# A two-layer graph attention network on one core: the order of loads at the start and ahead of layer 2's attention vectors

## The chip, the cores and the metric

The kernel runs on one core of one Trainium2 chip. The metric is the device time of one execution in microseconds. A core has a matrix engine (TensorE, PE in the profile, with its weight loads as PEld), a vector engine (VectorE, DVE), a scalar engine (ScalarE, ACT), a general one (GpSimd, POOL) and a synchronising one (SyncE, SP). Each runs its own instructions in program order, and they wait for each other by semaphores. Here SP's queue issues the plain loads and stores and the transposes by DMA, and POOL's queue the DMAs that add what they load to what stands in the destination (accumulating DMAs).

## The reference

512 nodes with 768 features, 16,896 edges (8,192 pairs in both directions and 512 loops), sorted by destination. Two graph attention layers, then a residual and a layer norm, all in float32:

```
def gat_layer(x, W, a_s, a_d, b, edge_index, concat):
    h = (x @ W).reshape(n, H, C)
    alpha_s = einsum('nhc,hc->nh', h, a_s);  alpha_d = einsum('nhc,hc->nh', h, a_d)
    e = leaky_relu(alpha_s[src] + alpha_d[dst], 0.2)
    e = exp(e - segment_max(e, dst)[dst])
    alpha = e / (segment_sum(e, dst)[dst] + 1e-16)
    return segment_sum(h[src] * alpha[:, :, None], dst).reshape(n, H * C) + b
h = elu(gat_layer(x, W1, a_src1, a_dst1, b1))      # 8 heads of 768
y = gat_layer(h, W2, a_src2, a_dst2, b2)           # 6144 to 768, one head
out = layernorm(x + y)
```

## The kernel before, in words

**The whole.** The edges are turned into a dense 512 x 512 matrix of counts (`cnt`), so that the attention of a head is a dense softmax with counts as weights and its message sum a dense product. Layer 1 is worked head by head: the projection x W1[h], the logits, the softmax, the attention's product, ELU, and the head's share of layer 2's projection, which is added into `h2`. All big products are done in float32 by schemes that trade multiplications for additions: 7 products of halves in place of 8 (`by_halves`, P1 to P7), or 15 of thirds. The sums of weights that these need are made on DVE, or by accumulating DMAs on POOL, the sums of activations on DVE. The order of all instructions on all engines is written out by hand (`manual_schedule`); no scheduler moves them.

**The projection of head 0 and its loads (lines 232 to 266).** The tiles `w1r` hold W1[0] as a lower and an upper half of rows (lo, hi), each with a left and a right half of columns (L, R). The loop at L251 and L252 issues the right halves: first block and rest of lo R, then hi R (576 KB). `sums_by_dma` (L254 to L264) then loads, on SP, the bases of the sums t2 (w1t2, from hi R) and t4 (w1t4, from hi L), 576 KB each (L259), and gives back two additions for POOL: t2 += t1 (L261) and t4 += t2 (L262). The attention rows a_s, a_d of head 0 follow (`load_a`, L224). `weight_sums` (L557), called in the second batch below, makes t1 = lo L + lo R on DVE (L559), then issues the first addition, a third accumulating load that makes lo R + hi R in place (L561), and the second addition. In the program's order the products (`multiply`, L426) of head 0 are P1, P2, P6, P7, P4, P5, P3 in pairs of halves of rows (i = 0, 1), six matmuls of the profile each; head 0 itself is worked in an order of its own, by a list of items. The same helper is called again for the last block of W2 with the same tiles (slot "w1").

**The front end (L273 to L384).** `keep_warm` issues matmuls on zeros so that TensorE is not idle while the first loads come. `nodes` is an iota; `offsets` (L366) a table of small numbers copied from it by DVE. The edge indices arrive as int32 (`idx_i`), are cast to float on DVE (`idx_f`, L367) and transposed on PE (L373), after six transposes of x (`turn_x`, L311), whose results ACT copies into `xT` (L312). From the transposed indices DVE and POOL make the parts of the one-hots (`fold`, `low`, `rel`, `two`, `weight`, L377 to L384).

**The counting (L732 to L888).** The count matrix is a sum of products of one-hots: 32 destinations by 256 sources for each chunk of 128 edges (`count`, L782). Source one-hots are made on DVE by comparison (L756, "ours") or on ACT by a sign (L754, "theirs"); destination one-hots on DVE for a quarter of the chunks at a time (`destinations`, L734 and L735). The loop over nine batches (L814 to L888) runs these beside the products of head 0: in each, first the quarter's destinations, then the source one-hots for the next batch, the list `extra` of sums and logits, some products with their emptying from PSUM, and at the end the counting matmuls of this batch. The list at L814 gives how many one-hots of each kind a batch takes. `inside` (L738) sums up how many edges lie in the block that their chunk is taken to cover; the sum decides whether a general pass is run afterwards.

**The step from head 0 to head 2's projection (h = 0 of the loop at L1229 on).** During the attention product of head 0 and layer 2's product, SP's queue holds, in this order: `load_w1(2)`, `load_a(2)` (a_s and a_d of head 2, each a row spread over 128 partitions, 384 KB, L224), the four loads of `attended(0)` (L1211 to L1214: 128 rows of W2's last block, a_src2 and a_dst2), then the transposes by DMA of the normalised weights (`turn_out`, L969), and then the three parts of `load_second(1)` (L153, L147, L161). Tiles with one buffer are reused, so that a load of a_d waits until DVE has done its last logit with the old a_d (L435). `turn_out` scales a tile on ACT, splits its 16-bit halves on ACT (L967) and issues the transpose on SP; `turn_in` joins the halves on ACT (L972). Then follows the projection of head 2 (L426, in `by_halves`): its P1 is emptied from PSUM by ACT (L465), its P2 by ACT too (L466), the others by DVE (L467 to L471). PSUM gives these products two banks of their own at that point, so that P2 can start when ACT has emptied P1. Between them DVE makes the sums of the next head's operands, the store of x's sums goes out on SP (L1148), and after P4 DVE takes the logits of head 2 (L444) with a_s and a_d. The functions `times` of `attended` (L1217) multiply the loaded rows on DVE to give layer 2's attention vectors.

Of the kernel before, what the change touches and what calls it, by code (L numbers as in the profile page):

```python
# [39 lines left out]
def gat_pass(  # L40
# [179 lines left out]
    def load_a(h, a_s, a_d):  # L220
        A[h] = []
        for name, a in (("a_s", a_s), ("a_d", a_d)):
            v = wpool.tile([P, D], F32, name=name)
            nc.sync.dma_start(v, row_bcast(a))  # L224
            A[h].append(v)
# [8 lines left out]
    def block(m, r, cols):  # L234
        return m[r * HK * P:(r + 1) * HK * P, cols].rearrange("(k p) d -> p k d", p=P)
# [12 lines left out]
    b1_rows = ohp.tile([H * DC, P], F32, name="b1_rows")  # L248
    nc.sync.dma_start(b1_rows, b1.rearrange("(j p) -> j p", p=P))
    W1[0].append(w1_halves[1])  # L250
    for r, ks in ((0, slice(0, 1)), (0, slice(1, HK)), (1, slice(0, HK))):  # L251
        nc.sync.dma_start(W1[0][r][:, ks, R], block(w1_0, r, R)[:, ks])  # L252

    def sums_by_dma(W_, m, slot):  # L254

        lo_, hi_, t1_ = W_
        t2, t4 = (w1_halves[j] if slot == "w1" else wpool.tile([P, HK, HALF], F32, name=f"{slot}t{j}") for j in (2, 4))
        for t_, cols in ((t2, R), (t4, L)):
            nc.sync.dma_start(t_, block(m, 1, cols))  # L259

        additions = [lambda: nc.gpsimd.dma_start(t2, t1_, accum_op=ALU.add),  # L261
                     lambda: nc.gpsimd.dma_start(t4, t2, accum_op=ALU.add)]  # L262
        return dict(P1=lo_[:, :, L], P2=hi_[:, :, L], P3=hi_[:, :, R], P4=t4, P5=t1_, P6=t2,
                    P7=lo_[:, :, R]), additions  # L264
# [5 lines left out]


    zeros = ohp.tile([P, 512], BF16, name="zeros")
    nc.vector.memset(zeros, 0.0)  # L273
    idle = bc.tile([P, 512], F32, name="bc")

    def keep_warm(n):
        for _ in range(n):
            nc.tensor.matmul(idle, zeros[:, :P], zeros, start=True, stop=True)

    keep_warm(7)  # L280
    nodes = ohp.tile([P, N], F16, name="nodes")
    nc.gpsimd.iota(nodes, pattern=[[1, N]], base=0, channel_multiplier=0,
                   allow_small_or_imprecise_dtypes=True)
# [23 lines left out]
    def turn_x(t, r):  # L307

        ps = mm.tile([P, 512], F32, name="mm")
        for k in range(HK):  # L310
            nc.tensor.transpose(ps[:, k * P:(k + 1) * P], x_sb[:, t, (r * HK + k) * P:(r * HK + k + 1) * P], ident)  # L311
        nc.scalar.copy(xT[:, r * HK:(r + 1) * HK, t * P:(t + 1) * P],  # L312
                       ps[:, :HALF].rearrange("p (k n) -> p k n", n=P))
# [4 lines left out]
    if general:  # L318
        nc.vector.tensor_copy(idx_f, idx_i)
        idx = ohp.tile([P, 2, EC], F32, name="idx")  # L320
        psi = tr.tile([P, 512], F32, name="tr")
        for j in range(2):
            for r in range(2):
                nc.tensor.transpose(psi[:, (2 * j + r) * EH:(2 * j + r + 1) * EH], idx_f[:, j, r, :],
                                    ident[:EH, :EH])
        nc.vector.tensor_copy(idx, psi[:, :2 * EC].rearrange("p (j c) -> p j c", j=2))
    else:

        B = 32
        blocks = []
        for c in range(EC):
            m = (c + 0.5) * P * N / E
            b = int(m // B)
            slack = 2 + 16 * (m / N * (1 - m / N)) ** 0.5
            lo, hi = b - (m - b * B < slack), b + ((b + 1) * B - m < slack)
            blocks.append(range(max(lo, 0), min(hi, N // B - 1) + 1))
        assert max(map(len, blocks)) <= 2


        QC = EC // NT
        QW = QC + QC % 2
        base = ohp.tile([P, EC], F32, name="base")
        two = ohp.tile([P, NT, QW], F16, name="two")
        rel = ohp.tile([P, NT, QW], F16, name="rel")
        weight = ohp.tile([P, 3, NT, QW], BF16, name="weight")

        def fill(values, put):
            lo = 0  # L350
            while lo < EC:
                hi = lo + 1
                while hi < EC and values[hi] == values[lo] and hi % QC:
                    hi += 1
                put(lo, hi, float(values[lo]))
                lo = hi

        fill([b[0] * B for b in blocks], lambda lo, hi, v: nc.gpsimd.memset(base[:, lo:hi], v))
        fill([len(b) > 1 for b in blocks],
             lambda lo, hi, v: nc.gpsimd.memset(two[:, lo // QC, lo % QC:lo % QC + hi - lo], v))  # L360
        if QW > QC:
            nc.gpsimd.memset(rel[:, :, QC:], -1.0)
            nc.gpsimd.memset(two[:, :, QC:], 0.0)
            nc.gpsimd.memset(weight[:, :, :, QC:], 0.0)
        offsets = ohp.tile([P, B, QW], F16, name="offsets")
        nc.vector.tensor_copy(offsets, nodes[:, :B].unsqueeze(2).to_broadcast([P, B, QW]))  # L366
        nc.vector.tensor_copy(idx_f, idx_i)  # L367
        turn_x(0, 0)
        turn_x(1, 0)
        psi = tr.tile([P, 512], F32, name="tr")  # L370
        for j in range(2):
            for r in range(2):
                nc.tensor.transpose(psi[:, j * EC + r * EH:j * EC + (r + 1) * EH], idx_f[:, j, r, :], ident[:EH, :EH])  # L373
        quarters = lambda v: v.rearrange("p (q c) -> p q c", c=QC)
        fold = ohp.tile([P, EC], F32, name="fold")
        low = ohp.tile([P, EC], F32, name="low")
        nc.vector.tensor_scalar(fold, psi[:, EC:2 * EC], float(HN), -float(HN), op0=ALU.is_ge, op1=ALU.mult)  # L377
        nc.vector.tensor_tensor(low, psi[:, EC:2 * EC], fold, op=ALU.add)
        nc.vector.tensor_tensor(rel[:, :, :QC], quarters(psi[:, :EC]), quarters(base), op=ALU.subtract)
        nc.gpsimd.tensor_scalar(weight[:, 2, :, :QC], quarters(fold), -(DIGIT - 1) / HN, 1.0, op0=ALU.mult, op1=ALU.add)  # L380
        nc.vector.scalar_tensor_tensor(two, rel, float(B), two, op0=ALU.is_ge, op1=ALU.mult)
        nc.vector.scalar_tensor_tensor(rel, two, -float(B), rel, op0=ALU.mult, op1=ALU.add)
        nc.gpsimd.tensor_tensor(weight[:, 1], weight[:, 2], two, op=ALU.mult)
        nc.gpsimd.tensor_tensor(weight[:, 0], weight[:, 2], weight[:, 1], op=ALU.subtract)  # L384
# [54 lines left out]
    def half(t, j, h=0):  # L439
        return lambda: half_logits(h, t)[j]()  # L440
# [273 lines left out]
    if not general:  # L714
# [81 lines left out]


        turns = {3: [(2, 0), (3, 0), (2, 1), (3, 1)]}
        keep_warm(1)
        found = const.tile([P, 1], F32, name="found")  # L800
        wholes = len(items)

# [2 lines left out]
        def ask():  # L805
            nc.vector.tensor_scalar(flag, pst[:1, :1], -1.0, float(E), op0=ALU.mult, op1=ALU.add)

        ahead_of = {1: [lambda: B1.update(weight_sums()), ask, s1]}
        extra = {1: [s2, s4], 3: [s3], 5: [half(0, 0), half(0, 1), half(1, 0)],
                 6: [half(2, 0), half(3, 0)], 7: [half(1, 1), half(2, 1)]}  # L810
        B1 = {}
        wants = [3, 6, 8, 10, 12, 14, 16, 18]
        batches = []
        for ours, theirs in ((16, 0), (6, 8), (8, 8), (13, 4), (13, 4), (13, 4), (13, 3), (13, 2), (4, 0)):  # L814
            take = [order[k][:m] for k, m in ((False, ours), (True, theirs))]
            del order[False][:ours], order[True][:theirs]
            batches.append(take[0][:ours // 2] + take[1] + take[0][ours // 2:])
        assert not any(order.values())
        pos, made, quarter, waiting, masks = 0, set(), EC // NT, [], []
        for n, batch in enumerate(batches):  # L820
# [58 lines left out]
                rank(q[1], 1)  # L879
            if n == 0:  # L880
                waiting.pop()()
                inside()
                pst = mm.tile([P, 512], F32, name="mm")
                nc.tensor.matmul(pst[:1, :1], found, ones, start=True, stop=True)
            if n == 3:
# [352 lines left out]
    for h in range(H - 1):  # L1238
# [14 lines left out]
        if h == 0:  # L1253
            GA, gsums = left(gT, gS)
            finish = near_first(0, AA, BB, [*rsums, lsums[3]], {(0, 1): [half(2, 0, 1)], (1, 1): sources[:1], (2, 1): [*sources[1:], *row, targets[0]]})
            load_w1(2)()
            load_a(2, a_src1[2], a_dst1[2])
            attend = attended(0)
            pairs = by_halves(h2, GA, B2)
            for m, _ in pairs[:2]:  # L1260
# [20 lines left out]
            for n in range(2, 7):  # L1281
                (m0, e0), (m1, e1) = pairs[2 * n:2 * n + 2]
                m0()
                m1()
                if n in (3, 5):
                    e0()
                if n < 6:
                    scored(n - 2)
                if n in (3, 4):
                    half(n - 1, 1, 1)()  # L1290
                if n < 5:
                    score(n - 1)
                if n == 6:
                    turn_in(0)
                    out_by_dma(2)
                if n not in (3, 5):
                    e0()
                if 3 < n < 6:
                    out_by_dma(n - 4)
                if n == 6:  # L1300
                    out_by_dma(3)
                    B2, sums2, load_pairs, load_first, load_rest = load_second(1)
                    load_pairs()
                    load_first()
                    load_rest()
                e1()
                if n < 5:
                    fold_count(n - 1)
# [294 lines left out]
```

## Time and profile before

| | |
|---|---|
| time, median of 3 runs | 625.62 us |
| lowest and highest | 623.74 and 625.76 us |
| the profiled execution | 625.87 us |
| its span, first to last instruction | 624.1 us |
| its mean granted TensorE clock | 0.995 |
| instructions | 8551 |
| moved by DMA | 129.46 MB, mean 207 GB/s |

How to read the rows. In a timeline a row has the start in us, the duration, the engine, the line, the operation, the tiles written and read with their shapes, the count of instructions joined in the row, and in brackets the idle time of the engine just before and what ended it. "SPq" and "POOLq" are the issues of DMAs by the sequencers of these engines: their duration is that of issuing, not of the transfer. In the chain of waits, a row has start, duration and what it was; a DMA row goes from issue to landing. In a list of waits, three numbers follow the name: the sum in us, the number of times, and the longest. In a table of stretches, the columns are the stretch, its length, then busy time and count of PE, PEld, DVE, ACT and POOL, then TensorE's granted clock, the share of the DMA engines' time, and GB/s. TensorE's float32 matmul of 128x384 takes several passes and about 0.32 us; twelve of them are one product of two halves of rows.

### The profile page before, as it was taken

The numbers are of one execution on the slowest core, as the hardware profiler recorded it, in microseconds if no ns is written. First come the engines' busy times: TensorE is split into PE (matmuls) and PEld (weight loads), VectorE is DVE, ScalarE is ACT, GpSimd is POOL, SyncE is SP. The second block draws the span as 40 slices with busy tenths as digits, with TensorE's granted clock in tenths as the row PEclk, the third lists the DMA queues.
The fourth block names the chain that finished last, engine by engine and source line by source line (L and its number), as shares of the span: only waits on it lengthen the run. The fifth ranks groups of instructions, "written<-read, shape, count | busy, mean of one in ns | idle before, by whom it ended". The sixth has DMA issues, their size and how long they took to land.

```text
span 624.1 us, 8551 instructions
## 1 busy us (share of the span) xinstructions
PE 611.6 (98%) x2765; PEld 483.4 (77%) x2765; DVE 525.1 (84%) x1137; ACT 333.6 (53%) x607; POOL 150.7 (24%) x188
## 2 busy tenths in 40 slices
PE   9999999999999999999999999999999999999995
PEld 5555685556888888888888888888888888886553
DVE  7989979868899878977798779977898778978785
ACT  4656867630658146751658146751758146754361
POOL 2310011032342234323342134323342223010000
PEclk9999999989999999999999999999999999999999
DMA  8994777899999999999899799999999995690042
GB/s 282 329 234 79 202 181 237 205 264 265 221 209 140 318 259 209 189 274 221 235 226 176 276 243 244 185 275 229 231 223 176 312 267 115 120 253 20 17 77 79
DMA packets 109569, 129.46 MB, mean 207 GB/s; under 512 B 41622, under 2 KB 90446, under 8 KB 108750
## 3 DMA queue, kind: packets, MB, share of 16 engines
q1 hardware_dynamic: 75518, 91.35, 47.7%
q0 software_dynamic: 33568, 36.90, 38.1%
q10 hardware_dynamic: 432, 0.59, 0.3%
q8 instruction: 24, 0.39, 0.3%
q14 instruction: 27, 0.22, 0.1%
HBM read 99.84 MB, written 2.90 MB: 165 GB/s over the span
## 4 chain that ended last, share of the span: by engine, by line
PE 89%; DMA 5%; DVE 3%; ACT 1%; issue 1%; SPq 0%; DVEq 0%; ACTq 0%; POOLq 0%
PE mm L500 46%; PE mm L1035 17%; PE mm L426 13%; PE mm L1075 6%; PE mm L1549 3%; PE held L426 2%; DMA w1t<-w1t 2%; DMA w1t<-in_L_gnn_W_dram 1%; DMA zr<-pS 1%; DVE scr L435 1%; PE tr L782 1%; DMA w1r<-in_L_gnn_W_dram 1%; DMA hs<-in_x_dram 1%; DVE q L681 0%; DVE cnt L698 0%
## 5 line engine op out<-in xcount | busy, mean ns | idle before, releaser
L506 ACT ACTIVATE hs<-mm 128x512 f32<-128x512 f32 x30 | 17.9, 596 | 86.0 <-PE mm L500 85.7
L1035 PE MATMUL mm<-PT,hs 128*128 128x256 f32 x216 | 52.5, 379 | 0.0
L513 DVE TENSOR_TENSOR hs<-hs,mm 128x512 f32<-128x512 f32 x45 | 30.9, 686 | 22.3 <-PE mm L500 22.2
L685 ACT ACTIVATE q<-q,nmax 128x512 f32<-128x512 f32 x32 | 23.1, 721 | 49.0 <-DVE nmax L681 48.7
L511 POOL DMA_DIRECT2D h<-pass x22 | 26.5, 1319 | 82.5 <-ACT pass L510 82.5
L1035 PEld LDWEIGHTS mm<-PT,hs 128*128 128x128 f32 x216 | 41.0, 190 | 5.8
L513 DVE TENSOR_TENSOR h<-h,mm 128x512 f32<-128x512 f32 x56 | 38.3, 683 | 6.3 <-PE mm L500 5.7
L972 ACT COPY PT<-zr 128x1024 uint16<-128x1024 uint16 x34 | 39.3, 1155 | 6.4 <-DMA zr<-pS 5.3
L500 PE MATMUL mm<-w2r,xT 128*128 128x256 f32 x160 | 37.8, 379 | 0.0
L500 PE MATMUL mm<-w2r,gT 128*128 128x256 f32 x160 | 37.1, 379 | 0.0
L1035 PE MATMUL mm<-pS,gS 128*128 128x256 f32 x144 | 37.0, 379 | 0.0
L135 POOL DMA_DIRECT2D w1t<-in_L_gnn_W_dram x18 | 27.3, 1537 | 30.5 <-DMA w1t<-in_L_gnn_W_dram 27.5
L500 PE MATMUL mm<-w1t,hs 128*128 128x256 f32 x144 | 34.1, 380 | 0.0
L500 PE MATMUL mm<-w1r,hs 128*128 128x256 f32 x144 | 34.1, 379 | 0.0
L500 PE MATMUL mm<-w1r,gS 128*128 128x256 f32 x144 | 34.0, 379 | 0.0
L500 PEld LDWEIGHTS mm<-w2r,gT 128*128 128x128 f32 x160 | 30.3, 190 | 4.4 <-issue 0.3
L500 PEld LDWEIGHTS mm<-w2r,xT 128*128 128x128 f32 x160 | 30.4, 190 | 4.1
L500 PEld LDWEIGHTS mm<-w1t,hs 128*128 128x128 f32 x144 | 27.3, 190 | 3.9 <-ACT absent L510 0.2
L1035 PEld LDWEIGHTS mm<-pS,gS 128*128 128x128 f32 x144 | 27.4, 190 | 3.7
L500 PEld LDWEIGHTS mm<-w1r,hs 128*128 128x128 f32 x144 | 27.2, 190 | 3.8 <-DVE hs L1194 0.2
L500 PEld LDWEIGHTS mm<-w1r,gS 128*128 128x128 f32 x144 | 27.3, 190 | 3.7
L1039 ACT COPY u<-mm 128x256 f32<-128x256 f32 x18 | 6.7, 372 | 42.9 <-PE mm L1035 42.9
(308 smaller groups left out, 1577.6 us busy)
## 6 DMA issues: line engine op xcount, KB each, us to landing
w2r<-in_L_gnn_W_dram SPq DMA_DIRECT2D x48, 384.0 KB
w1r<-in_L_gnn_W_dram SPq DMA_DIRECT2D x43, 384.0 KB
gT<-xd SPq DMA_DIRECT2D x5, 1280.0 KB
w1t<-in_L_gnn_W_dram SPq DMA_DIRECT2D x24, 256.0 KB
h<-pass POOLq DMA_DIRECT2D x22, 256.0 KB, 4.5
w1t<-in_L_gnn_W_dram POOLq DMA_DIRECT2D x18, 256.0 KB, 5.5
w2t<-in_L_gnn_W_dram SPq DMA_DIRECT2D x15, 256.0 KB
w2t<-in_L_gnn_W_dram POOLq DMA_DIRECT2D x15, 256.0 KB, 9.0
```

The lines of the kernel that those rows point to most:

```text
L135: nc.gpsimd.dma_start(o, i, accum_op=ALU.add)
L426: nc.tensor.matmul(ps[:, :HALF], A_[p][:, k, i * P:(i + 1) * P], B_[p][:, k, :], start=start and k == 0, stop=k == HK - 1, skip_group_chec ...
L500: nc.tensor.matmul(bank[chain][:, i * TH:(i + 1) * TH], A_[p][:, k, i * P:(i + 1) * P], B_[p][:, k, :], start=first and i == k == 0, stop= ...
L506: nc.scalar.activation(out(o), ps, AF.Copy, scale=sign)
L511: nc.gpsimd.dma_start(out(o), part, accum_op=ALU.add)
L513: nc.vector.tensor_tensor(out(o), out(o), ps, op=ALU.add if sign > 0 else ALU.subtract)
L685: nc.scalar.activation(q, q, AF.Exp, bias=nmax, scale=-1.0, accum_out=dens[t])
L972: nc.scalar.copy(PT.rearrange("p s n -> p (s n)").bitcast(U16).rearrange("p (s n h) -> p s n h", s=NT, h=2)[:, :, t * P:(t + 1) * P, :], p ...
L1035: nc.tensor.matmul(bank[p][:, :HN], A_[p][:, k, c * P:(c + 1) * P], B_[p][:, k, :], start=over is None and k == 0, stop=k == 1, skip_group ...
L1039: nc.scalar.copy(u, part("P1"))
L1075: nc.tensor.matmul(banks[c, p][:, :HN], A_[p][:, k, c * P:(c + 1) * P], B_[p][:, k, :], start=over is None and k == 0, stop=k == 1, skip_g ...
L1549: nc.tensor.matmul(ps[:, :cols.stop - cols.start], PT[:, s, t * P:(t + 1) * P], h2[:, s, cols], start=(s == 2), stop=(s == 1))
```

## The change

Seven edits. In SP's queue, the load of hi R of head 0's weights goes from ahead of t2's base to behind it; as the insertion is in `sums_by_dma` under the slot "w1", the helper's second use for the last block of W2 now issues that load as well. Further on, `load_a(2)` goes from ahead of `attended(0)` to behind the last part of `load_second(1)`. On the front end: the zeros are cleared in two parts, and the warm-up is 8 matmuls of 128 columns and 5 of 512 in place of 7 of 512, with the single later one dropped; `offsets` is copied by ACT in place of DVE; the transposes of the indices stand ahead of those of x on PE. In the batches, `inside` goes from behind the first products to ahead of them, and of the chunks whose one-hots DVE makes, two go from the second batch to later ones: (6, 8) becomes (4, 8), (13, 3) and (13, 2) become (14, 3) and (14, 2).

```
-    for r, ks in ((0, slice(0, 1)), (0, slice(1, HK)), (1, slice(0, HK))):
-        nc.sync.dma_start(W1[0][r][:, ks, R], block(w1_0, r, R)[:, ks])
+    for ks in (slice(0, 1), slice(1, HK)):
+        nc.sync.dma_start(W1[0][0][:, ks, R], block(w1_0, 0, R)[:, ks])
...
-        for t_, cols in ((t2, R), (t4, L)):
+        loads = [(t2, R), (t4, L)]
+        if slot == "w1":
+            loads.insert(1, (hi_[:, :, R], R))
+        for t_, cols in loads:
             nc.sync.dma_start(t_, block(m, 1, cols))
...
-    nc.vector.memset(zeros, 0.0)
+    nc.vector.memset(zeros[:, :P], 0.0)
+    nc.vector.memset(zeros[:, P:], 0.0)
...
-    def keep_warm(n):
+    def keep_warm(n, cols=512):
         for _ in range(n):
-            nc.tensor.matmul(idle, zeros[:, :P], zeros, start=True, stop=True)
-    keep_warm(7)
+            nc.tensor.matmul(idle[:, :cols], zeros[:, :P], zeros[:, :cols], start=True, stop=True)
+    keep_warm(8, P)
+    keep_warm(5)
...
-        nc.vector.tensor_copy(offsets, nodes[:, :B].unsqueeze(2).to_broadcast([P, B, QW]))
+        nc.scalar.copy(offsets, nodes[:, :B].unsqueeze(2).to_broadcast([P, B, QW]))
         nc.vector.tensor_copy(idx_f, idx_i)
-        turn_x(0, 0)
-        turn_x(1, 0)
         psi = tr.tile([P, 512], F32, name="tr")
         for j in range(2):
             for r in range(2):
                 nc.tensor.transpose(psi[:, j * EC + r * EH:j * EC + (r + 1) * EH], idx_f[:, j, r, :], ident[:EH, :EH])
+        turn_x(0, 0)
+        turn_x(1, 0)
...
-        keep_warm(1)
...
-        extra = {1: [s2, s4], 3: [s3], 5: [half(0, 0), half(0, 1), half(1, 0)],
+        extra = {0: [inside], 1: [s2, s4], 3: [s3], 5: [half(0, 0), half(0, 1), half(1, 0)],
...
-        for ours, theirs in ((16, 0), (6, 8), (8, 8), (13, 4), (13, 4), (13, 4), (13, 3), (13, 2), (4, 0)):
+        for ours, theirs in ((16, 0), (4, 8), (8, 8), (13, 4), (13, 4), (13, 4), (14, 3), (14, 2), (4, 0)):
...
             if n == 0:
                 waiting.pop()()
-                inside()
...
             load_w1(2)()
-            load_a(2, a_src1[2], a_dst1[2])
             attend = attended(0)
...
                     load_first()
                     load_rest()
+                    load_a(2, a_src1[2], a_dst1[2])
```

## The prediction

> **What bounds the kernel now.** I read the page's first part, then what TensorE waits for over the whole span, then the stretch between the first and the last hole.
>
> ```profile
> span 624.1 us, 8551 instructions
> PE 611.6 (98%) x2765; PEld 483.4 (77%) x2765; DVE 525.1 (84%) x1137; ACT 333.6 (53%) x607; POOL 150.7 (24%) x188
> ```
> ```profile
> PE mm L426 <- ACT hs L465: 2.5, 1, 2.5
> ...
> PE held L426 <- issue: 0.7, 1, 0.7
> PE held L426 <- DMA w1t<-w1t: 0.6, 1, 0.6
> PE mm L426 <- ACT os L754: 0.4, 1, 0.4
> ```
> ```profile
> 130.00:571.00 441.00, 441.00 (x2001) 377.96 (x1999) 370.85 (x747) 231.27 (x422) 133.21 (x111) 1.00 0.96 224
> ```
>
> PE is busy for 98% of the span. The second fence is what PE waits for in the whole program, but for the wait ahead of its first instruction: one wait of 2.5 us and three small ones. The third (stretch, sum, busy time and count of PE, PEld, DVE, ACT, POOL, then granted clock, DMA share, GB/s) says that from 130 to 571 us PE is never idle, at full clock. So a microsecond taken out of PE's holes ahead of 130 comes off the end whole, as long as no new hole opens. One taken out of another engine is worth nothing. The change touches two places that hold such holes, the first 40 us (A) and the stretch around 126 us (B); the rest is bookkeeping.
>
> **A: the first weights' sums.** Columns of the timeline: start, duration, engine, line, what it does, count, idle time before and its releaser.
>
> ```profile
> 8.53 0.86 SPq L252
> 9.43 8.72 DMA w1t<-in_L_gnn_W_dram
> 18.78 9.74 DMA w1t<-w1t
> ```
> ```profile
> 17.60 4.03 PE L426 MATMUL mm<-w1t,xS 128*128 128x384 f32 x12
> 19.17 1.74 DVE L756 TENSOR_SCALAR os<-nodes,low 128x256 bf16<-128x256 f16 x8
> 19.57 1.71 POOL L561 DMA_DIRECT2D w1r<-in_L_gnn_W_dram  x1
> 22.86 4.11 PE L426 MATMUL mm<-w1r,xS 128*128 128x384 f32 x12 [0.42 <-ACT os L754]
> 28.57 4.14 PE L426 MATMUL held<-w1t,xS 128*128 128x384 f32 x12 [0.60 <-DMA w1t<-w1t]
> 34.36 4.11 PE L426 MATMUL held<-w1r,xT 128*128 128x384 f32 x12 [0.73 <-issue]
> ```
> ```profile
> w1r<-in_L_gnn_W_dram POOLq DMA_DIRECT2D x1, 576.0 KB, 14.7
> ```
> ```profile
> 14.00:16.00 2.00, 1.97 (x29) 1.50 (x30) 1.39 (x4) 1.92 (x6) 0.00 (x0) 1.00 1.07 383
> ```
>
> The chain goes by the load of t2's base (issued at 9.43, landed at 18.15), then by POOL's addition t2 += t1 (L261, 18.78 to 28.52), whose landing starts PE's product at 28.57. Right behind it POOL issues L561 at 19.57; with its 14.7 us it lands at 34.27, and the product of 34.36, put down to "issue" by the profile, starts just then. The change takes one load of 576 KB (hi R, issued by L252 at 8.53) from ahead of t2's base. By the bandwidth row 576 KB (589,824 bytes) at 383 GB/s are 1.54 us; by SP's issue alone it would be 0.9 us (9.43 to 8.53). The queue is saturated, so I take 1.54. Both additions shift by it: L261's landing to about 27.0, L561's to about 32.7. Ahead of them the product at 22.86 is held by DVE, which makes eight one-hots (1.74 us, 0.22 each) before its operand; two one-hots fewer are 0.44, so it starts at about 22.4. Then PE reaches the next product at about 27.3 (22.4, 4.0 of matmul, 0.26 for L702 and about 0.6 of counting), behind the landing; and the last waits for L561 at 32.7. A is worth 34.36 - 32.75 = **1.6**; I take 1.5, as the groups of counting before the product at 34.36 are of 32 and not of 28 matmuls. Its bounds are 0.9 (issue alone) and 1.9 (L561 in a thinner queue). The two later one-hots (13 to 14 twice, 0.44) go to DVE behind 36 us, where PE waits for nothing; if that cover were missing they would cost 0.4.
>
> **A's front end.** The number table leaves DVE (2.37) and goes to ACT.
>
> ```profile
> 2.19 2.37 DVE L366 COPY offsets<-nodes 128x1088 f16<-128x1088 f16 x1
> 4.58 0.42 DVE L367 CAST idx_f<-idx_i 66x512 f32<-66x512 int32 x1
> ```
> ```profile
> 1.27 3.17 PE L278 MATMUL bc<-zeros 128*128 128x512 bf16 x7 [1.27 <-DVE zeros L273]
> 4.36 1.53 PE L311 MATMUL mm<-ident,hs 128*128 128x128 f32 x6
> 5.67 0.65 PE L373 MATMUL tr<-ident,idx_f 66*128 66x66 f32 x4
> 6.54 2.89 PE L644 MATMUL held<-w1r,xT 128*128 128x384 f32 x8
> 13.15 1.76 PE L311 MATMUL mm<-ident,hs 128*128 128x128 f32 x12
> 114.23 1.04 ACT L967 COPY pS<-q 128x1024 uint16<-128x1024 uint16 x1
> ```
> ACT's nearest row, a copy of 128x1024 two-byte elements, takes 1.04; ACT has nothing to copy before the first transposes are done, so the table costs nothing between 1.0 and DVE's 2.37. What changes is PE's order: index transposes (L373) ahead of those of x (L311). They need the cast, which cannot end before about 5.0 (4.58 + 0.42; how much the table held it back the trace doesn't tell, since the two rows touch). The warm-up now has 8 matmuls of 128 and 5 of 512 columns: at 3.17 / 7 = 0.45 each for 512 and a quarter for 128 that is 3.2, from about 1.1 to 4.2. So PE has a hole of some 0.8 us where it had none. The transposes of x start at about 5.65 in place of 4.36, and L644, no longer behind the dropped warm-up matmul, at about 6.95 in place of 6.54: 0.4 late. By itself that is hidden: between 17.60 and 34.36 PE has 0.42 + 0.60 + 0.73 = 1.75 of waits in the rows above, of which A's 1.5 takes none beyond what the landings dictate. It costs nothing as long as the landings at 27.0 and 32.7 come last. That `inside` moves ahead of one DVE addition puts two instructions under 0.5 us in front of work that was waiting anyway: nothing.
>
> **B: layer 2's attention rows.**
>
> ```profile
> 112.75 0.33 SPq L224 DMA_DIRECT2D a_d<-in_L_gnn_a_dst_dram  x1
> ...
> 117.79 1.04 ACT L967 COPY pS<-q 128x1024 uint16<-128x1024 uint16 x1
> ...
> 121.30 1.16 ACT L972 COPY PT<-zr 128x1024 uint16<-128x1024 uint16 x1 [2.47 <-DMA zr<-pS]
> ...
> 125.77 0.85 ACT L465 COPY hs<-mm 128x384 f32<-128x384 f32 x2
> ...
> 126.30 5.81 PE L426 MATMUL mm<-w2r,xT 128*128 128x384 f32 x12 [2.53 <-ACT hs L465]
> ```
> ```profile
> 115.42 5.86 DMA zr<-pS
> ```
> ```profile
> 71.15 1.23 SPq L969 DMA_TRANSPOSE zr<-nr  x1
> 74.29 1.16 ACT L972 COPY PT<-zr 128x1024 uint16<-128x1024 uint16 x1 [0.54 <-DMA zr<-nr]
> ```
> ```profile
> 126.29:129.71 3.42, 3.41 (x6) 1.90 (x7) 2.75 (x4) 1.40 (x2) 0.00 (x0) 0.50 0.94 113
> ```
>
> The load of a_d waits on SP until DVE is done with the old one (112.75). The four loads of `attended` stand behind it, and the transposes behind those: issued at 115.42 by the chain of waits, landed at 121.28, 5.86 later, because they share the queue with loads issued in the two microseconds before. At 71.15 a transpose with little ahead of it lands 3.14 after its issue. ACT sits idle for 2.47 until the landing, runs its chain, and frees PE's bank (L465) only at 125.77; PE, done at 126.30 - 2.53 = 123.77, resumes at 126.30. The hole then costs a second time: the next 3.41 us run at a granted clock of 0.50, and twelve matmuls take 5.81 in place of 4.03 (the product at 17.60 has the same shape and count), 1.78 more.
>
> With a_s and a_d out of the way, `attended`'s loads wait for nothing behind 105 and land before the transposes are issued at 115.4 (pS is ready at 114.23 + 1.04). Those then land at about 118.6 (3.14, as at 71.15), but ACT is busy until 117.79 + 1.04 = 118.83. So the whole chain shifts by at most 121.30 - 118.83 = 2.47; I take 2.35. PE resumes at 123.95, 0.2 after it was done, the clock stays, and B's gross gain is 2.35 + 1.78 = **4.1**.
>
> [...]
>
> **What B adds: a_s and a_d late.**
>
> ```profile
> 146.29 0.96 DVE L444 SCALAR_TENSOR_TENSOR scr<-hs,a_s 128x768 bf16<-128x768 f32 x1
> ...
> 147.43 4.03 PE L426 MATMUL mm<-w2r,xS 128*128 128x384 f32 x12
> 148.17 0.55 DVE L470 TENSOR_TENSOR hs<-mm,hs 128x384 f32<-128x384 f32 x1
> ```
> ```profile
> 138.00:142.00 4.00, 4.00 (x14) 2.33 (x13) 3.65 (x7) 0.00 (x0) 1.20 (x1) 1.00 1.18 243
> 142.00:146.00 4.00, 4.00 (x14) 2.41 (x13) 3.22 (x6) 0.00 (x0) 3.04 (x3) 1.00 1.24 196
> ```
>
> They now stand on SP behind the three transposes, a fourth, and the loads L153, L147 and L161 for head 2, and ahead of the xd store, which waits for work of DVE at 144 anyway. In before the rate falls from 243 to 196 GB/s between the two rows, where SP's loads end and POOL's accumulating loads (L135) are left alone: at about 142.6 by my estimate, so at about 140.3 after the shift. At 243 GB/s the 384 KB of each of a_s and a_d take 1.6 and at half of it, shared evenly with POOL, 3.2. Their rows of 3 KB should give them most of it, as by the code the loads beside them move rows of 1 KB; I put a_s at 142.2 (141.7 to 143.5) and a_d at 144.1 (142.9 to 146.5). DVE wants them at 146.29 - 4.1 = 142.2 and one instruction (1.0) later: that one is about 1.0 late. Behind L444 on DVE stands L470, which frees the bank for PE's next product but one; in before it ends at 148.72, and PE wants it at 149.37 (half of the product begun at 147.43), 0.65 of slack. The stall is 1.0 - 0.65 = 0.4, by the ends 0 to 2.7. B's net: 4.1 - 0.4 = **3.7**, from 1.4 to 4.3.
>
> The last head's use of the same helper now loads hi R twice (576 KB between its two bases); its users come 40 us later, and the loads around it wait for PE: nothing, or at most those 1.54.
>
> **The sum.** The profiled execution took 625.87 (1.8 beside its span), a little above the median of 625.62 (623.74 to 625.76). 625.87 - 1.5 - 3.7 = **620.7**.
>
> **Rivals.**
> (1) *Front hole delays the clock*. PE's matmuls before 6.8 run at about half rate (six transposes in 1.53; later twelve in 1.76), with no hole from 1.27 on. With a new hole of 0.8, the full clock may come one window of 3.41 later, as the 0.50 row has it behind 126.29: 1.7 of matmul time lost, plus the 0.4. Against the slack above, A shrinks from 1.5 to about 0.5: 621.7. [...]
> (2) *a_s and a_d come later still*. The new wait then takes back B: at a_d's late end, a net of 1.4, so 623.0. From a stall above about 2.5 PE's clock drops again (1.78). For the program to be **slower** than before, stall and drop have to exceed A's 1.5 and B's gross 4.1, so the stall 5.6 - 1.78 = 3.8. That needs a_d to land after 143.2 + 0.65 + 3.8 = 147.7, its 768 KB with a_s at under 106 GB/s from 140.3, less than half of the 243 in the row.
> (3) *The transposes land as late as before*, since something else than the four loads holds them (POOL's additions in the queue, say): B is nothing, A stays, 624.4. That the 3.14 at 71.15 is there at all speaks against it.
> (4) *t2's base comes sooner and nothing follows*, as POOL's 9.74 stretches to fill the queue: A only 0.4 by the one-hots, 621.8.
>
> **How the numbers follow.** Forecast 0.50; rival 1 0.22; rival 2 without a loss 0.10, with one 0.04; rival 3 0.08; rival 4 0.06. The range goes from 625.87 - 1.9 - 4.3 = 619.7, less 0.3 for a single run, to 623.4, which takes in rivals 1, 4 and the mild form of 2: 619.4 to 623.4. About 0.3% is what a measurement of this kernel can tell from no change, 1.9 us, so faster is below 623.7: forecast, 1, 2 mild and 4, 0.88, less a little for unnamed trouble, 0.86. Same 0.09, slower 0.05.
>
> **What would show it.** Right: PE's product at 126.30 starts at or before 124 less A's shift, with no granted clock under 1.0 behind it; the transposes land about 3.1 after issue; t2's addition issues at about 17.2 and the product of 34.36 starts at 32.7. Wrong: a wait of DVE on a_d above 1.7 at L444 followed by a PE hole; a granted clock or pace at half behind 6.8; ACT's L972 still waiting 2 us for zr.

## The result, and the profile after

| | before | after |
|---|---|---|
| median | 624.81 us (16 runs, 623.03 to 626.77) | 622.38 us (16 runs, 619.97 to 623.18) |
| ratio of the times | | 0.9953, 95% interval 0.994 to 0.9967 |
| profiled execution, span | 625.87, 624.1 | 622.47, 620.7 |
| mean granted clock | 0.995 | 0.997 |

The change makes the kernel 2.43 us faster in the median, 0.47% (0.33 to 0.6). The forecast was 620.7 in a range of 619.4 to 623.4: direction and range hold, the size only in part. 5.2 was forecast from the profiled execution (625.87 to 620.7). By the profiled executions 3.40 came; by the medians 2.43, just under half, since the profiled execution of before lies 1.06 above its median.

From here on line numbers are those of the kernel shown; in the changed kernel L426 is L431, L444 is L449, L470 is L475, L465 is L470, L644 is L649; in the experiments they shift by up to as much.

What PE waits for in the whole of the changed kernel:

```profile
PE bc L282 <- DVE zeros L276: 1.1, 1, 1.1
PE tr L376 <- DVE idx_f L372: 0.9, 1, 0.9
PE mm L431 <- DVE hs L475: 0.8, 1, 0.8
PE mm L431 <- ACT hs L470: 0.3, 1, 0.3
```

The wait of 2.5 on ACT is down to 0.3, the two on t2's additions are gone, and there are two new ones: 0.9 on the indices' cast (the forecast's hole of 0.8) and 0.8 on a DVE addition behind a_d (forecast: 0.4). The front, in the timeline:

```profile
1.08 3.17 PE L282 MATMUL bc<-zeros 128*128 128x128 bf16 x13 [1.08 <-DVE zeros L276]
...
3.02 1.10 ACT L371 COPY offsets<-nodes 128x1088 f16<-128x1088 f16 x1
...
4.60 0.42 DVE L372 CAST idx_f<-idx_i 66x512 f32<-66x512 int32 x1 [2.33 <-DMA idx_i<-in_src_dram]
...
5.17 0.67 PE L376 MATMUL tr<-ident,idx_f 66*128 66x66 f32 x4 [0.92 <-DVE idx_f L372]
...
7.05 3.72 PE L649 MATMUL held<-w1r,xT 128*128 128x384 f32 x8
...
16.90 1.05 POOL L264 DMA_DIRECT2D w1t<-w1t  x1 [8.57 <-DVE flag L810]
...
18.93 4.03 PE L431 MATMUL mm<-w1t,xS 128*128 128x384 f32 x12
...
28.56 4.14 PE L431 MATMUL held<-w1t,xS 128*128 128x384 f32 x12
...
33.66 4.14 PE L431 MATMUL held<-w1r,xT 128*128 128x384 f32 x12
```

The cast is late because the indices land late (2.33 of idle time, released by their DMA), not because the table had held DVE. L649's eight matmuls take 3.72; they took 2.89 in before and 2.74 in the quickest runs below. If they ran at half pace first and then at full, the half pace lasted until about 9.0 (an estimate: 7.05 + 2 x (3.72 - 2.74)). The profile's granted clock reads 1.00 over the first 12 us of before and of the changed kernel, also where matmuls take nearly twice their time (six transposes of x take 1.49 from 5.63 on and 0.82 from 10.60 on), so "half clock" at the front is here always judged by this pace. So the product of 17.60 starts at 18.93, 1.33 later. t2's addition is issued at 16.90, 1.88 earlier, and none of the later products waits for a DMA any more: they follow PE's own work. The product of 34.36 starts at 33.66, 0.70 earlier, where 1.5 was forecast.

The stretch around 126, timeline and the transposes' row in the chain of waits:

```profile
118.48 1.16 ACT L975 COPY PT<-zr 128x1024 uint16<-128x1024 uint16 x1 [0.23 <-DMA zr<-pS]
...
123.47 4.14 PE L431 MATMUL mm<-w2r,xT 128*128 128x384 f32 x12 [0.28 <-ACT hs L470]
...
142.91 0.96 DVE L449 SCALAR_TENSOR_TENSOR scr<-hs,a_s 128x768 bf16<-128x768 f32 x1 [1.16 <-DMA a_s<-in_L_gnn_a_src_dram]
...
144.30 0.96 DVE L449 SCALAR_TENSOR_TENSOR scr<-hs,a_d 128x768 bf16<-128x768 f32 x1 [0.42 <-DMA a_d<-in_L_gnn_a_dst_dram]
...
145.80 2.20 PE L431 MATMUL mm<-w2r,xS 128*128 128x384 f32 x6 [0.77 <-DVE hs L475]
```
```profile
114.72 3.73 DMA zr<-pS
```

The transposes land 3.73 after their issue in place of 5.86, ACT waits 0.23 for them in place of 2.47, PE resumes after 0.28 of idle time in place of 2.53, and its twelve matmuls take 4.14 in place of 5.81. Then a_s and a_d come 1.16 + 0.42 = 1.58 late for DVE, and PE stands for 0.77.

The span's 3.40 by stage, from the starts of the same work in both timelines: to the product of 34.36, 0.70; from there to head 2's P1 (119.74 to 119.16), 0.12 lost; from P1 to the first attention product behind the projection (31.56 to 28.68), 2.88; behind it 0.07 lost. The last head's doubled load of hi R thus cost nothing that shows.

### The profile page after: what moved, and what is told of

It reads as the page before. It is cut to its first block, busy times and chain, and to the rows that moved or that the text cites. A ratio compares the mean times of both kernels' runs of the same rounds, so it can differ in the third digit from the quotient of the medians.

```text
span 620.7 us, 8565 instructions
## 1 busy us (share of the span) xinstructions
PE 610.5 (98%) x2770; PEld 483.2 (78%) x2770; DVE 522.7 (84%) x1137; ACT 335.1 (54%) x608; POOL 150.5 (24%) x188
## 4 chain that ended last, share of the span: by engine, by line
PE 89%; DMA 4%; DVE 4%; ACT 1%; issue 0%; SPq 0%; DVEq 0%; ACTq 0%
PE mm L505 46%; PE mm L1038 18%; PE mm L431 11%; PE mm L1078 6%; PE mm L1552 3%; PE held L431 2%; DMA a_d<-in_L_gnn_a_dst_dram 2%; DMA w1r<-in_L_gnn_W_dram 1%; PE tr L787 1%; PE held L649 1%; DVE scr L440 1%; DMA zr<-pS 1%; DMA idx_i<-in_src_dram 1%; PE mm L316 0%; ACT pS L970 0%
## 5 line engine op out<-in xcount | busy, mean ns | idle before, releaser
L505 PEld LDWEIGHTS mm<-w1t,hs 128*128 128x128 f32 x144 | 27.3, 190 | 3.9 <-ACT absent L515 0.2
L505 PEld LDWEIGHTS mm<-w1r,gS 128*128 128x128 f32 x144 | 27.3, 190 | 3.7
```

What stands on the lines that cost most here:

```text
L505: nc.tensor.matmul(bank[chain][:, i * TH:(i + 1) * TH], A_[p][:, k, i * P:(i + 1) * P], B_[p][:, k, :], start=first and i == k == 0, stop= ...
```

## The experiments

Each ran against the kernel before on its own chip: e1 to e4 on one, e5 to e8 on a second, e9 to e12 on a third. The changed kernel was run again beside e9 to e12 (as e11), but not beside the others, which are compared with it only through the ratios to before. In the table the ratio has its 95% interval; then, from one profiled execution each, the start and duration of the first eight matmuls of the projection (L644), the start of the product of 34.36, and the time from P1 of head 2's projection to the first attention product.

| kernel | median, before's | ratio | L644 | at 34.36 | P1 on |
|---|---|---|---|---|---|
| before | 624.81 | | 6.54, 2.89 | 34.36 | 31.56 |
| changed | 622.38, 624.81 | 0.9953 (0.994 to 0.9967) | 7.05, 3.72 | 33.66 | 28.68 |
| e1 rows only | 622.64, 625.39 | 0.9957 (0.9941 to 0.9972) | 6.31, 2.75 | 34.09 | 27.72 |
| e2 t2 only | 624.37, 625.39 | 0.998 (0.9967 to 0.9992) | 5.74, 2.74 | 32.19 | 31.43 |
| e3 front only | 626.86, 625.39 | 1.0023 (1.0007 to 1.0039) | 6.67, 2.85 | 33.69 | 33.10 |
| e4 no front | 621.59, 625.39 | 0.9949 (0.9931 to 0.9967) | 5.84, 2.74 | 31.85 | 27.46 |
| e5 hole filled | 620.61, 625.2 | 0.991 (0.9881 to 0.9939) | 6.48, 2.85 | 32.23 | 28.10 |
| e6 x first | 621.21, 625.2 | 0.9922 (0.9892 to 0.9953) | 5.57, 2.80 | 32.69 | 28.24 |
| e7 no batches | 621.66, 625.2 | 0.9931 (0.9902 to 0.9961) | 6.90, 3.68 | 33.57 | 28.32 |
| e8 filled at 126 | 625.25, 625.2 | 0.9992 (0.9969 to 1.0014) | 6.23, 2.74 | 33.24 | 31.60 |
| e9 filled less | 623.67, 625.74 | 0.9966 (0.9955 to 0.9977) | 6.55, 2.74 | 34.62 | 30.32 |
| e10 a earlier | 621.77, 625.74 | 0.993 (0.9911 to 0.9948) | 7.35, 4.16 | 34.40 | 28.19 |
| e11 changed again | 622.72, 625.74 | 0.9956 (0.9942 to 0.9971) | 7.21, 3.95 | 34.05 | 27.92 |
| e12 both mends | 620.52, 625.74 | 0.9918 (0.9902 to 0.9934) | 7.61, 3.85 | 34.36 | 27.51 |

**The parts one by one.** Theory 1 after the result: the rows' move and the sooner base are worth what was forecast, and the front end takes part of it back. The rival: the base is worth only the 0.7 seen, and the front end is neutral.

e1, before with one line moved:

```
-            load_a(2, a_src1[2], a_dst1[2])
...
                     load_rest()
+                    load_a(2, a_src1[2], a_dst1[2])
```

> The kernel before with one edit: load_a(2) goes behind load_second(1)'s last part in SP's queue. Theory 1 (B's parts are independent of A's, and every execution of before pays them): the product of 126.30 starts 2.5 earlier, its twelve matmuls take 4.1 in place of 5.81, and a_d, late, gives back 0.8: 3.4 less in the profile's span, and the same in the median. [...]

```profile
123.67 4.14 PE L426 MATMUL mm<-w2r,xT 128*128 128x384 f32 x12 [0.16 <-ACT hs L465]
...
143.13 4.24 PE L426 MATMUL mm<-w2r,xS 128*128 128x384 f32 x12
```
```profile
143.67 0.96 DVE L444 SCALAR_TENSOR_TENSOR scr<-hs,a_d 128x768 bf16<-128x768 f32 x1 [0.62 <-DMA a_d<-in_L_gnn_a_dst_dram]
```

In the profile P1 on is 31.56 - 27.72 = 3.84 shorter: the whole of the forecast's gross 4.1 but 0.3. a_d is 0.62 late for DVE, and PE's twelve matmuls of P3 take 4.24 in place of 4.03, without a hole in that row: the slack of 0.65 that the forecast gave it nearly held. The median moves by 0.43% (0.28 to 0.59), 2.7 us, less than the profile's; that interval leaves open how much of the 3.84 a typical execution of before pays.

e2, before with the order of the base's loads as changed (with the second use of the helper):

```
-    for r, ks in ((0, slice(0, 1)), (0, slice(1, HK)), (1, slice(0, HK))):
+    for ks in (slice(0, 1), slice(1, HK)):
...
+        if slot == "w1":
+            loads.insert(1, (hi_[:, :, R], R))
```

> The kernel before with one edit: hi R of head 0's weights loads behind t2's base (and, by the same helper, once more for the last block of W2). Theory 1 (the load order is worth 1.6 by itself, and the changed kernel lost half of it to its front end): the product of 34.36 starts at 32.7 to 32.9, 1.5 to 1.6 less in the span. Rival (the load order is worth only the 0.7 that the changed kernel shows at this product): 33.6 to 33.7, 0.7 less.

```profile
5.74 2.74 PE L647 MATMUL held<-w1r,xT 128*128 128x384 f32 x8
...
32.19 4.14 PE L429 MATMUL held<-w1r,xT 128*128 128x384 f32 x12
...
124.23 5.62 PE L429 MATMUL mm<-w2r,xT 128*128 128x384 f32 x12 [2.59 <-ACT hs L468]
```

The product starts 2.17 earlier than in before, but this execution also had the full pace sooner (L644 at 5.74, not 6.54). If that 0.80 carries through, 1.4 is the loads'; this split is a subtraction, not shown. Over the five profiles with the loads as before the product starts at 33.24 to 34.62; in the two with the sooner base and the old front (e2, e4) at 32.19 and 31.85, with no wait on a DMA. The median says 0.2% (0.08 to 0.33), 1.25 us. The step for A was about right in size. The rival, 0.7 less in the span, does not fit the profile; the interval in the median (0.5 to 2.1 us) leaves room for it.

e3, before with all else of the diff, no load moved:

> The kernel before with the front end's edits and the batches' alone (zeros and warm-up, ScalarE's number table, indices turned first, inside ahead of the products, chunks moved to later batches); loads as in before. Theory 1 (the front end delays PE by 1.3, which the late landings of before hide): the product of 17.60 starts at 18.9, those of 28.57 and 34.36 where they did, the median moves by under 0.4. Rival (the front end is neutral or a gain): the product of 17.60 starts at 17.6 or sooner, and the median falls by 0.4 or more.

```profile
17.69 4.03 PE L428 MATMUL mm<-w1t,xS 128*128 128x384 f32 x12
...
33.69 4.11 PE L428 MATMUL held<-w1r,xT 128*128 128x384 f32 x12 [0.67 <-issue]
...
127.32 5.76 PE L428 MATMUL mm<-w2r,xT 128*128 128x384 f32 x12 [4.12 <-ACT hs L467]
```
```profile
114.86 7.43 DMA zr<-pS
```

Both theories fall here: the front end alone is slower by 0.23% (0.07 to 0.39), 1.4 us, and not at the place that theory 1 named. In this execution the front did no harm (the product of 34.36 starts 0.67 sooner, and the eight matmuls take 2.85 behind a hole of 1.09), but the transposes landed 7.43 after their issue, and PE's hole at 126 grew to 4.12. e8, with the old front, shows 7.3 for the same transposes. So while the four loads stand ahead of them, this latency differs from execution to execution; whether the new front makes the long one more frequent isn't settled.

e4, the changed kernel with the front end and the batches of before, so e1 and e2 together:

> The changed kernel with the front end and the batches of before: both moves of loads, nothing else. Theory 1: the product of 34.36 starts at 32.7 to 32.9, and the whole is 0.8 to 1.0 faster than the changed kernel, 4.2 to 4.4 less than before in the span. Rival (the front end is neutral or a gain): as fast as the changed kernel or slower, 3.4 less than before or under that.

The product of 34.36 starts at 31.85 and P1 on takes 27.46, the shortest of all. The profiled execution took 619.66. The median is 0.51% less than before (0.33 to 0.69), the changed kernel's 0.47%: theory 1's extra 0.8 to 1.0 is not shown by the times of this kernel, which spread from 619.23 to 624.92. By ratios the parts e1, e2 and e3 add up to -0.43 - 0.20 + 0.23 = -0.40%, against -0.47 and (e11) -0.44. But e4, which is e1 and e2 together, came to -0.51 and not -0.63, only 0.04 below the changed kernel: what the front end costs in the median isn't settled by these.

**The hole behind the warm-up.** e5, e6 and e7 part the front end:

```
e5:  -    keep_warm(5)
     +    keep_warm(7)
e6:  +        turn_x(0, 0)
     +        turn_x(1, 0)
              psi = tr.tile([P, 512], F32, name="tr")
     ...
     -        turn_x(0, 0)
     -        turn_x(1, 0)
e7:  -        extra = {0: [inside], 1: [s2, s4], ...
     +        extra = {1: [s2, s4], ...
     (batches and the place of inside as before)
```

> The changed kernel with two more warm-up matmuls of 512 columns, so that PE works on until the cast of the indices has landed (0.85 of the hole of 0.92). Theory 1 (the hole keeps the clock at half beyond 6.8, and PE's late start is then the bound of the first 34 us): L649's eight matmuls take under 3.0, and the median is 0.8 to 1.2 less than the changed kernel's, so 3.3 to 3.7 less than before. [...]

> The changed kernel with x turned before the indices again, all else as changed. Theory 1 (the order of the transposes is what the front end costs): PE has no hole behind its warm-up, L649 starts at 6.5 or sooner, and the median is 0.8 to 1.4 less than the changed kernel's. Rival (the cost is in the batches or nowhere): within 0.5 of the changed kernel.

> The changed kernel with the batches and the place of inside as before; loads, warm-up, number table and the order of the transposes as changed. Theory 1 (the cost is the order of the transposes): within 0.5 of the changed kernel. Rival (moving one-hots to later batches and inside ahead of the products is what costs, by a fuller DVE up to 66 us): 0.8 to 1.4 less than the changed kernel.

The first rows of PE's timeline in e5, then e6, then e7:

```profile
1.08 3.73 PE L282 MATMUL bc<-zeros 128*128 128x128 bf16 x15 [1.08 <-DVE zeros L276]
5.14 0.44 PE L376 MATMUL tr<-ident,idx_f 66*128 66x66 f32 x4 [0.34 <-DVE idx_f L372]
...
6.48 2.85 PE L649 MATMUL held<-w1r,xT 128*128 128x384 f32 x8 [0.24 <-ACT xT L317]
```
```profile
5.57 2.80 PE L649 MATMUL held<-w1r,xT 128*128 128x384 f32 x8
```
```profile
5.02 0.67 PE L376 MATMUL tr<-ident,idx_f 66*128 66x66 f32 x4 [0.77 <-DVE idx_f L372]
...
6.90 3.68 PE L649 MATMUL held<-w1r,xT 128*128 128x384 f32 x8
```

e5 is the test of the mechanism: the same kernel with two matmuls on zeros more, and the eight matmuls take 2.85. e6, without the hole by order, has L649 at full pace too; e7 keeps hole and slow L649. Over all profiles: of the six with a hole of 0.6 to 1.3 there (changed, e3, e7, e10, e11, e12), five run these matmuls at half pace for a time (3.68 to 4.16) and one not (e3, 2.85); of the other eight, which have at most 0.43 of idle time there in one piece, none does (2.74 to 2.89). So the hole doesn't delay the clock each time, but mostly. With half pace the product of 34.36 starts at 33.57 to 34.40 where the base came sooner, without it at 31.85 to 32.69 (e2, e4, e5, e6): some 1.7 between the middles, about all that A was to bring. The 1.7 holds both costs of the hole, PE's later start and the half pace.

What this costs the median is less sure. e5's interval (0.9881 to 0.9939) lies just below the changed kernel's (0.994 to 0.9967), but e7, which keeps hole and half pace, also comes out 1.4 better than the changed kernel by the ratios: the rival's figure, not theory 1's. On this chip the kernel before spreads from 622.97 to 629.93, so all three ratios may be flattered, and whether the batches cost anything stays open. Against e7 on the same chip e5 is 1.05 less and e6 0.45, and the times overlap.

**The half clock behind the hole of 126.** e8 and e9 fill the hole of before with matmuls on x, whose result is dropped:

```
             for n in range(14):
+                if h == 0 and n == 2:
+                    filler = bc.tile([P, 512], F32, name="bc")
+                    for _ in range(7):        # e9: 4
+                        nc.tensor.matmul(filler[:, :HALF], xT[:, 0, :P], xT[:, 0, :HALF], start=True, stop=True)
                 pairs[n][0]()
```

> The kernel before with seven matmuls of 128x384 on x's transposed tile, into a bank that nothing else uses, between P1 and P2 of head 2's projection: 2.25 of the hole of 2.53 at 126 are filled with work whose result is dropped. Theory 1 (the hole costs twice, the second time by the half clock behind it): PE's product of 126.30 starts where it did, its twelve matmuls take 4.1 in place of 5.81, and the median falls by 1.5 to 1.8. [...] If idle time alone cost: no change.

> As the filled kernel before it, with four matmuls in place of seven: each took two passes of 0.32, so that seven were 4.51 and longer than the hole; four are 2.6. Their result is dropped. Theory 1 (the half clock behind the hole costs 1.78 in every execution with a hole over 2): from P1's start to the first attention product 29.8 in place of 31.5 in the profile, and the median falls by 1.3 to 1.8. Rival (the half clock is paid in some executions only): the median falls by 0.4 to 1.2. If idle time alone cost: no change.

```profile
122.50 4.68 PE L1410 MATMUL bc<-xT 128*128 128x384 f32 x14
126.10 0.85 ACT L465 COPY hs<-mm 128x384 f32<-128x384 f32 x2
127.01 4.03 PE L426 MATMUL mm<-w2r,xT 128*128 128x384 f32 x12
```
```profile
123.86 2.74 PE L1410 MATMUL bc<-xT 128*128 128x384 f32 x8
126.99 4.14 PE L426 MATMUL mm<-w2r,xT 128*128 128x384 f32 x12 [0.38 <-ACT hs L465]
```

e8's filling was sized wrongly: each matmul counts twice in the rows (x14), so that it took 4.5, 2.0 more than a hole like before's; that is about what the clock gained, and the median shows no change. In the execution shown the transposes landed late (7.3) and ACT came to P1's bank only at 126.10, so that there the filling overran the hole by little. e9's 2.6 leaves 0.38 of hole; the product behind takes 4.14, not 5.81, and the median falls by 0.34% (0.23 to 0.45), 2.1 us, with no useful work done sooner. The half clock is a cost of its own, about what the forecast charged (1.78), and the median pays it.

It isn't paid in every execution, though. In before's profile the granted clock is below 1.00 at 126 and in the last 14 us (0.90 there), and the mean is 0.995; the profiles with no half clock at 126 have means of 0.997 and 0.998. A stretch of 3.41 at half clock takes 3.41 / 2 / 624 = 0.0027 off the mean, so an execution with 0.998 has no room for one at 126 beside the end. On e5's chip 7 of the 18 executions of before have 0.998, with a median of 623.78, and 10 have 0.995 or less, with 626.58; on the other two chips 2 of 25 and 1 of 13 have 0.998. So e9's rival has a part: most executions of before pay, and some do not.

**a_d's lateness, and both mends.** e10 is the changed kernel with load_a(2) one step sooner, e11 the changed kernel again, e12 e10 with e5's warm-up:

```
                     load_first()
+                    load_a(2, a_src1[2], a_dst1[2])
                     load_rest()
-                    load_a(2, a_src1[2], a_dst1[2])
```

> The changed kernel with load_a(2) ahead of load_second(1)'s last part in place of behind it: the same bytes, four loads of 384 KB and the L161 pair behind a_s and a_d. Theory 1 (the hole of 0.8 to 0.9 ahead of P3 is a_d's lateness): a_d lands by 139, PE has no hole at 145, and the median is 0.5 to 0.9 less than the changed kernel's. Rival (DVE is late for other reasons, or the loads put off are missed instead): within 0.3.

> The changed kernel itself on this chip, for the comparison with the two beside it, and a second profile. Theory 1 (the hole behind the warm-up makes the full clock late in some executions): times fall into two groups, about 620.3 and 622.8, and L649 starts at half clock or not. Rival (one state, spread by the transfers): one group.

> The changed kernel with both mends: two more warm-up matmuls and load_a(2) ahead of the last part of load_second(1). Theory 1: 1.0 to 1.5 less than the changed kernel from the first and 0.5 to 0.9 from the second, 619.8 to 620.4 in the median, in one group. Rival (the two holes were cover for something else): no better than the better of the two alone.

```profile
143.08 0.96 DVE L449 SCALAR_TENSOR_TENSOR scr<-hs,a_s 128x768 bf16<-128x768 f32 x1
...
144.08 0.96 DVE L449 SCALAR_TENSOR_TENSOR scr<-hs,a_d 128x768 bf16<-128x768 f32 x1
```
```profile
124.77 4.14 PE L431 MATMUL mm<-w2r,xT 128*128 128x384 f32 x12 [0.83 <-ACT hs L470]
...
144.22 4.03 PE L431 MATMUL mm<-w2r,xS 128*128 128x384 f32 x12
```
```profile
5.73 0.67 PE L376 MATMUL tr<-ident,idx_f 66*128 66x66 f32 x4 [0.63 <-DVE idx_f L372]
...
7.61 3.85 PE L649 MATMUL held<-w1r,xT 128*128 128x384 f32 x8
```

The first two fences are e10: DVE takes a_d one instruction behind a_s, and P3's twelve matmuls (4.03) have no hole. In this execution the transposes took 4.28, and PE stood for 0.83 ahead of P2; no half clock followed (4.14). So P1 on is no shorter than e11's (28.19 against 27.92), and the gain rests on the median: 0.95 less than e11's, the intervals overlap by little. e11 repeats the changed kernel: 0.9956, L649 at half clock (3.95), 0.33 of hole ahead of P3; its six times (621.79 to 623.91) do not fall into the two groups expected. e12 (620.52; 619.8 to 620.4 was expected) is 2.2 us faster than e11 on the same chip, and their intervals are apart: the two mends together are shown, each of them alone is not. With e5 it is the quickest version. The last fence shows its limit: in that execution the cast came only at 5.7, so that even the longer warm-up left a hole of 0.63 and the clock was late.

In e5 one more wait appears in the list of what PE waits for:

```profile
PE mm L505 <- DMA gT<-xd: 0.7, 1, 0.7
```

It is the reload of x's sums ahead of the product at 204.89, which in before was in time. PE's coming sooner doesn't explain it alone: in e4 PE reaches this product at 203.51 and doesn't wait.

## Why the prediction was right or wrong

- **That PE's holes are what counts, and carry to the end**: right. From the product of 34.36 to P1 took 85.37 to 85.61 in every kernel, and behind the first attention product 472.5 to 473.9. The condition "no new hole" is not idle: a_d's wait, and e5's 0.7 at 205.
- **A, the sooner base**: about right in size where it stands alone (1.4 by subtraction in the profile, 1.25 by the median; forecast 1.5). In the changed kernel it fell to 0.70, as the front end came late: rival 1, which gave 0.5.
- **A's front end at nothing**: this is the step that failed. The hole was foreseen (0.8; measured 0.92), the delay of L644 too (6.95; 7.05). The forecast said that it costs nothing while the landings of 27.0 and 32.7 come last. But by its own working PE reached the product of 28.57 at 27.3, behind the landing, so that no cover was left there; and of the 1.75 of waits it had A take 1.5, so that less was left than the 0.4 that L644 comes late. The landings also came sooner than reckoned: the first by 26.40, when POOL's next addition, which waits for it, starts, and the second at about 31.8 (17.69 at issue and 14.1 to landing). PE came last, and at half pace until about 9.0, one of the forecast's own signs of being wrong. I gave this 0.22; the profiles with a hole show it in five of six. Without the hole the eight matmuls are fast in all eight profiles (2.74 to 2.89), with it in one of six (2.85 in e3, 3.68 to 4.16 in the others). Why e3's hole of 1.09 left the pace as it was, no run shows. In the profile A lost 0.8 to this; what the median lost stays open (0.04% by e4, 0.23% by e3, 0.43% by e5).
- **B's first gain, the transposes**: right. 2.25 by PE's idle time (2.53 to 0.28), forecast 2.35. They landed 3.73 after issue, not 3.14, so that ACT waited 0.23 for them. In e3 and e8, with the loads ahead, the same landing took 7.4 and 7.3: how much there is to gain differs from execution to execution.
- **B's second gain, the clock**: right, and shown apart from the first by e9: 1.67 here (5.81 to 4.14), forecast 1.78. It was charged as certain, from one profile; by the mean clocks some executions of before don't pay it, which may be one reason why the median fell by less than the profile.
- **B's new wait**: right in place, too small in size. a_d came about when forecast (144.2; 144.1), but DVE was ready for a_s at 141.75 in place of 142.2 and a_s itself was 1.16 late, so that a_d's start was 1.58 late in place of 1.0. PE stood for 0.77, and P3 as a whole took 1.04 longer (142.93 to 147.84, 3.87 in before), in place of 0.4. That their rows of 3 KB give a_s and a_d most of the queue was the author's estimate; no run tests it. In e1 and e4, with the old front, a_d is only 0.6 late and PE has no hole; with the new one PE has a hole of 0.33 to 0.77 in each of five (changed, e5, e6, e7, e11). The transfer is no slower there: a_d lands 11.7 to 12.2 after its issue in all seven. Its issue on SP is later, 12.4 to 13.1 behind P1's start in the five, 11.7 and 12.0 in the two. What in the new front delays the issue stays open.
- **Rivals**: 3 and 4 are out by e1 and e2. What came is rival 1 with a larger new wait. Rival 2's slower form is not near: at a_d's lateness of 1.58 the hole is 0.8, far from 3.8.

## What to carry to other kernels

A reordering that lets one engine start a side job sooner is paid for by whoever is put behind it: look at when the input of the job that goes first lands, and fill any hole that this makes in TensorE, also in a stretch that other waits seem to hide. When two edits take away waits that covered a third edit's delay, that delay must be added up against the path as it will be, not as it was. A hole in TensorE is to be priced with the half clock that may follow: here behind one of 0.6 to 1.3 us at the start in five of six profiles, behind those of 2.5 to 4.1 us at 126 in each of three (1.6 to 1.8 on twelve matmuls), and not behind e10's 0.83. Since that half clock is not paid in every execution, a forecast from one profile should ask whether its execution is a typical one.

## What the runs showed of the hardware

- A hole of 0.6 to 1.3 us in the first 6 us left TensorE at half pace until beyond 8.5 us in five of six profiles, by an estimate from the time that eight matmuls took (3.68 to 4.16, and 2.74 to 2.89 in the eight profiles without such a hole; the granted clock reads 1.00 there in the changed kernel). A hole of 2.5 to 4.1 us at 126 was followed by half clock in each of the three profiles that had one unfilled (twelve matmuls in 5.81 in before, 5.62 in e2, 5.76 in e3, against 4.03); one of 0.83 in e10 was not (4.14). By the mean clocks (0.998, where that half clock takes an estimated 0.0027 off), 10 of 56 executions of before on the three chips had no room for it.
- The first DMA transpose landed 3.6 to 4.3 us after issue with the four loads out of its way (3.73 in the changed kernel, 3.60 in e1, 4.28 in e10), and 5.9 to 7.4 with them ahead (5.86 in before, 7.43 in e3, about 7.3 in e8 and 6.4 in e9 by ACT's rows).
- The cast of the edge indices, which waits for their landing, started between 4.45 (e7) and 5.16 us (e12) in kernels with the same first loads.
